# The last batch of a cross-attention kernel: batch six's norms, softmax and weights two steps earlier, and the group sums dealt to the engines anew

## The chip, the core and the metric

The kernel runs on one core of a Trainium2 chip. The engines are called by the profile's names: PE multiplies matrices, DVE, ACT and POOL are the three engines for vectors, activations and general work, SP issues the transfers. The metric is the device time of one execution in microseconds (us). Three runs of the kernel before took 431.64 to 433.29 us, with a median of 432.96. The profile comes from one more execution, which took 434.03 us.

## The reference: what is computed

Eight batches of 112 queries (320 channels, 20 heads of 16) attend to 375 context rows of 512 channels, of which the last four are "prompt" rows. Beside the usual attention over the 371 text rows, each head compares the context that it has gathered with the prompt rows and mixes the four prompt values by that. All of it is float32. Cut to what matters:

```python
probs_t = softmax(q @ k_t^T * attn_scale)              # 112 x 371, per head
text_out = probs_t @ v_t
qsem = l2norm(probs_t @ text_ehs)                      # 112 x 512, per head
sem = qsem @ l2norm(ip_ehs)^T                          # 112 x 4
fused = q @ k_ip^T * attn_scale + 0.5 * sem
probs_ip = softmax(fused) * spatial_mask
out = (text_out + probs_ip @ v_ip) @ W_out + b_out + x
```

## The kernel before, in words

**Groups.** A step is one batch and one group of four heads, so a batch has five steps, g = 0 to 4. The kernel never forms the 112 x 512 rows of `qsem`. For a head with unnormalised probabilities p it needs only the norm of p @ context, which is the square root of p G p, where G is the Gram matrix of the context rows. Half of the symmetric G, with its off-diagonal part doubled, stands in the tile `u` beside the prompt columns, a column of ones and the head's values.

**One step.** `scores` (L686, PE) makes the scores of one head into a PSUM bank `ps_s`; `probabilities` takes their maximum (L709, DVE, tile `nmx`), the exponential (L712, ACT, tile `p`) and copies the four prompt scores out (L714, ACT, `ipl`), after which the bank is free. `sent` (L721, SP) moves p into the ring buffer `xg`, `transposed` (L729, DVE) turns it into `xgT`, in two halves in the last batch. `multiplied` (L748, PE) multiplies `xgT` with `u` into four banks `ps_qd`, one for each head, in 12 rounds j of four matrix products. The four heads use different quarters of the array's rows, and so run side by side. Before a group's products, `placed` (L655, POOL) copies that group's values into `u`, in three pieces; it may overwrite a piece only when the group before has used it, and the next group's products wait for it.

**Sums of a group.** What stands in a bank `ps_qd` is then used in two ways. The last 21 columns are copied to `pvs` by ACT (`value_sums` L761, or L778 inside `shared`). The first 371 are multiplied with p and summed, which gives the squared norm in `ss`. There are two ways to do that: `reduced` (L794) does it in one DVE instruction, with a short second one that reads the sum; `shared` has ACT copy the bank to memory (L779), POOL multiply (L783) and ACT sum (L787). `shared` is a generator with three pieces, so that the caller decides where each lands. In the last batch the first n heads of a group go to `shared`, the rest to `reduced`, with n = 3, 3, 2, 0 for g = 0 to 3.

**Finishing a batch.** `finish` is a generator, too. Piece 1: z squared, the larger of `ss` and that, the reciprocal of z (L835, L837, L848, DVE), and the division of the text output (L843, POOL). Piece 2: the square root on ACT (L852) and a load of ACT's table for the exponential (L853). Piece 3: reciprocal, product with the prompt sums, scaling, maximum, difference (L859 to L865, DVE, tile `fu`). Piece 4: the exponential (L869, ACT). Piece 5: sum, reciprocal and weights w (L873 to L877, DVE). Piece 6: the weights' transpose (L883, PE) and its copy (L889, ACT). Piece 7: the attention output and the weighted prompt values in one bank `ps_a` (L897, L900, PE), for batch six behind some filler products (L439). Then a copy (L910, ACT), the output projection `ps_o` (L917, PE), the sum with the residual (L928, DVE) and the transfer (L931, SP). The prompt values stand in a block diagonal matrix `bd`, which `own_channels` (L635, L638, POOL) makes out of a loaded one; `with_bias` (L808, POOL) adds the bias to the residual.

**The end of the kernel.** Batches are numbered 0 to 7. In the last batch's loop (b = 7) the pieces of `finish(6)` are interleaved with the steps: piece 1 inside step 1, piece 2 after step 1, pieces 3 and 4 after step 2, piece 5 after step 3. Batch seven is finished in two parts: its first 16 heads by the same `finish` (pieces 1 to 4 after step 3), its last four by `last_heads` (L1010 to L1057), behind step 4. `last_keys` (L560) and a last projection of queries (L344) stand ahead of step 1's products. Step 4's scores are made inside step 1, in banks of the pool `ps_qd`, and step 2's products use the same banks.

**What sets the order.** In this part every engine's order is written out by hand: an engine does its instructions in the order of the Python calls, and waits at each for what it needs. PSUM has eight banks in three pools: `ps_qd` with four, `ps_sc` and `ps_mm` with two each. A pool hands its banks out in turn, and a new tile waits until the last use of the bank's old one is over. Odd groups of the last batch take their product banks from `ps_mm` and `ps_sc`.

## Time and profile before

| | |
|---|---|
| median of three runs | 432.96 us (431.64 to 433.29) |
| profiled execution | 434.03 us, its span 432.2 us |
| mean granted PE clock | 0.991 of full speed |
| PE busy | 422.2 us (98%) |
| DVE busy | 327.5 us (76%) |
| ACT busy | 188.9 us (44%) |
| POOL busy | 110.0 us (25%) |

The span runs from the first to the last instruction of the profiled execution; about 1.8 us of that execution's time lie around it. All times of the form 409.81 are microseconds from the start of the span. In rows of a timeline the columns are start, duration, engine, line, operation, tile written and tiles read with their shapes, and how many instructions are merged in the row; in brackets stands the idle time ahead of it with what ended it. The chain of waits follows the work back from the last instruction, at each step to what released it. A view by stretches gives the busy time of each engine in each stretch, with counts in parentheses, then the granted PE clock as a share of full speed, the busy share of the DMA engines and their GB/s. The last batch's products begin at 384.65 us, and the last transfer of the result is issued at 429.36 us.

### The profile page before, as it was taken

To read this page: it belongs to the slowest core of one execution; us is meant where nothing else is said; L and a number is where in the kernel's file an instruction comes from. 1 tells how busy PE (TensorE), PEld (TensorE's weight loads), DVE (VectorE), ACT (ScalarE), POOL (GpSimd) and SP (SyncE) were. 2 spreads that over 40 slices of the span, in tenths; PEclk is the share of its full clock that TensorE was granted. 3 is DMA by queue.
4 is the path that set the end of the run, shared out by engine and by line. 5 is a ranking of instruction groups with operands and counts; after the bars stand their busy time and mean duration, and the time that the engine had idled before them with its cause. 6 is when DMAs were issued, how large, how long until landed. Compare 5 with 4: busy or idle time off the path is not lost.

```text
span 432.2 us, 13976 instructions
## 1 busy us (share of the span) xinstructions
PE 422.2 (98%) x5521; PEld 331.1 (77%) x5521; DVE 327.5 (76%) x674; ACT 188.9 (44%) x656; POOL 110.0 (25%) x274
## 2 busy tenths in 40 slices
PE   8999999999999999999999999999999999999986
PEld 8867868778777877888777877888776887788873
DVE  5038569786987879887897878897878877887872
ACT  2344342345434363336344353335434463455852
POOL 5310101112161213421160212511151120526600
PEclk9999999999999999999999999999999999999988
DMA  8676665786555865676645946566656447562200
GB/s 250 181 192 207 144 167 159 170 191 143 150 135 143 200 174 149 146 173 143 168 122 138 208 116 177 134 143 158 160 151 148 120 125 186 143 163 81 60 2 28
DMA packets 57631, 64.28 MB, mean 149 GB/s; under 512 B 18448, under 2 KB 51592, under 8 KB 57566
## 3 DMA queue, kind: packets, MB, share of 16 engines
q1 hardware_dynamic: 56934, 62.42, 57.0%
q8 instruction: 44, 0.72, 0.8%
q10 hardware_dynamic: 632, 0.96, 0.7%
q14 instruction: 21, 0.17, 0.1%
HBM read 18.67 MB, written 5.32 MB: 56 GB/s over the span
## 4 chain that ended last, share of the span: by engine, by line
PE 88%; DMA 4%; DVE 4%; ACT 2%; SPq 1%; issue 1%; DVEq 0%; ACTq 0%
PE ps_qd L748 42%; PE ps_v L578 13%; PE ps_k L544 9%; PE ps_g L502 7%; PE ps_s L686 5%; PE ps_q L344 3%; PE ps_o L962 2%; DMA xg<-p 2%; DMA vipx<-vipd 2%; DVE xgT L729 1%; PE ps_g L458 1%; PE ps_o L917 1%; DVE junk L794 1%; DMA ct<-in_ctx_dram 1%; PE ps_k L560 1%
## 5 line engine op out<-in xcount | busy, mean ns | idle before, releaser
L748 PE MATMUL ps_qd<-u,xgT 32*112 32x328 f32 (+11 forms) x3840 | 220.6, 353 | 0.6 <-DVE xgT L729 0.6
L748 PEld LDWEIGHTS ps_qd<-u,xgT 32*112 32x112 f32 x3840 | 187.9, 172 | 34.0 <-issue 10.4
L729 DVE STREAM_TRANSPOSE xgT<-xg 128x1536 f32<-128x1536 f32 (+1 forms) x45 | 119.2, 2665 | 7.6 <-DMA xg<-p 7.5
L712 ACT ACTIVATE p<-ps_s,nmx 112x371 f32<-112x371 f32 x156 | 84.9, 582 | 78.1 <-DVE nmx L709 62.0
L709 DVE TENSOR_REDUCE nmx<-ps_s 112x1 f32<-112x371 f32 x160 | 77.5, 528 | 43.8 <-PE ps_s L686 42.0
L794 DVE CUSTOM_DVE_ANT_0 junk<-ps_qd,p 112x371 f32<-112x371 f32 x146 | 79.2, 542 | 17.7 <-PE ps_qd L748 1.6
L686 PE MATMUL ps_s<-kT,qm 32*112 32x375 f32 (+1 forms) x320 | 64.9, 483 | 0.1
L655 POOL COPY u<-vr 128x64 f32<-128x64 f32 x120 | 26.0, 238 | 150.4 <-PE ps_qd L748 98.8
L578 PE MATMUL ps_v<-wv_sb,ctxT 128*128 128x384 f32 (+1 forms) x192 | 63.6, 480 | 0.0
L578 PEld LDWEIGHTS ps_v<-wv_sb,ctxT 128*128 128x128 f32 x192 | 35.2, 190 | 19.7
L544 PE MATMUL ps_k<-ctxT,wk_sb 128*128 128x371 f32 x136 | 46.3, 483 | 0.2 <-DVE ctxT L425 0.2
L761 ACT COPY pvs<-ps_qd 112x21 f32<-112x21 f32 x152 | 16.3, 190 | 63.9 <-PE ps_qd L748 62.0
L544 PEld LDWEIGHTS ps_k<-ctxT,wk_sb 128*128 128x128 f32 x136 | 24.9, 190 | 15.2 <-POOL ct L138 0.5
L502 PE MATMUL ps_g<-ctxT 128*32 128x375 f32 (+11 forms) x672 | 30.4, 333 | 0.0
L686 PEld LDWEIGHTS ps_s<-kT,qm 32*112 32x112 f32 x320 | 26.6, 170 | 4.8 <-ACT kT L551 2.0
L502 PEld LDWEIGHTS ps_g<-ctxT 128*32 128x32 f32 x672 | 27.7, 110 | 2.0
L714 ACT COPY ipl<-ps_s 112x4 f32<-112x4 f32 x140 | 23.6, 169 | 0.0
L353 DVE TENSOR_SCALAR qm<-ps_q,emask 128x224 f32<-128x224 f32 (+1 forms) x25 | 9.0, 394 | 17.5 <-PE ps_q L344 17.5
L404 DVE STREAM_TRANSPOSE ctxT<-ct 128x512 f32<-128x512 f32 x18 | 20.0, 1111 | 1.3 <-DMA ct<-in_ctx_dram 1.3
L585 ACT COPY vext<-ps_v 128x384 f32<-128x384 f32 (+1 forms) x24 | 11.3, 469 | 22.1 <-PE ps_v L578 22.1
L475 POOL TENSOR_TENSOR ug<-ug,half 128x128 f32<-128x128 f32 (+1 forms) x24 | 10.5, 449 | 32.0 <-ACT ug L474 32.0
L937 POOL TENSOR_TENSOR wv<-vip,w 112x1280 f32<-112x1280 f32 x6 | 14.8, 2466 | 14.3 <-DVE w L877 14.3
(169 smaller groups left out, 326.0 us busy)
## 6 DMA issues: line engine op xcount, KB each, us to landing
xg<-p SPq DMA_DIRECT2D x156, 162.3 KB
u<-ug SPq DMA_DIRECT2D x124, 99.0 KB
ct<-in_ctx_dram SPq DMA_DIRECT2D x24, 176.0 KB
vr<-vd SPq DMA_DIRECT2D x32, 120.0 KB
vip<-vipd SPq DMA_DIRECT2D x6, 560.0 KB
vd<-vext SPq DMA_DIRECT2D x7, 320.0 KB
vd<-vext SPq DMA_DIRECT2D x7, 160.0 KB
out_dram<-ob SPq DMA_DIRECT2D x8, 140.0 KB
```

Of the source, the lines that this page charges most:

```text
L404: nc.vector.transpose(ctxT[:, :, c * P : (c + 1) * P].rearrange("p e (j i) -> p j e i", i=RG), ct[:, some, :].rearrange("p j (k e) -> p j ...
L502: nc.tensor.matmul(ps[c][q * RG : (q + 1) * RG, j * RG - c * P : T - c * P], ctxT[:, e, j * RG : (j + 1) * RG], ctxT[:, e, j * RG : T], st ...
L544: nc.tensor.matmul(ps[:, :TT], wk_sb[:, e, i * P : (i + 1) * P], s["ctxT"][:, e, :TT], start=(e == 0), stop=(e == NE - 1),)
L578: nc.tensor.matmul(ps[:, :w], ctxT[:, e, c * P : (c + 1) * P], wv_sb[:, e, :w], start=(e == 0), stop=(e == NE - 1),)
L655: nc.gpsimd.tensor_copy(v, dealt(b, c, s["vr"][:, c * QN : (c + 1) * QN, g, :]))
L686: nc.tensor.matmul(ps[:S, :w], qm[a * RG : (a + 1) * RG, i, r, j * S : (j + 1) * S], s["kT"][a * RG : (a + 1) * RG, i, :w], start=True, st ...
L709: nc.vector.tensor_reduce(nmx, ps[:S, :TT], AX.X, ALU.max, negate=True)
L712: nc.scalar.activation(s["p", g][:, a, :], ps[:S, :TT], AF.Exp, bias=nmx)
L714: nc.scalar.copy(s["ipl"][:, groups[g][a], :], ps[:S, TT:T])
L729: nc.vector.transpose(xT[:, j : j + n].rearrange("p j (k q) -> p q j k", q=QN), xg[:, :, j * RG : (j + n) * RG].rearrange("p q (j k) -> p ...
L748: nc.tensor.matmul(banks[a][:S, j * RG : UW], xT[a * RG : (a + 1) * RG, j, :S], region(b, c)[a * RG : (a + 1) * RG, q, j * RG - c * P :], ...
L794: nc.vector.tensor_tensor_reduce(out=junk, in0=ps[:S, :TT], in1=s["p", g][:, a, :], scale=1.0, scalar=0.0, op0=ALU.mult, op1=ALU.add, accu ...
```

## The change

All edits lie in the last batch's loop, apart from one new parameter.

- `value_sums` takes an end a1, so that it can copy some of a group's heads.
- Batch six is finished earlier. Piece 1 comes at the end of step 0 instead of inside step 1. Pieces 2 to 4 come ahead of step 1's products, behind a load of the square root's table, instead of after steps 1 and 2. Piece 5, the weights, comes inside step 1 instead of after step 3.
- Step 3's scores of heads 0 and 1 are made after round 3 of step 0 instead of after round 1, and heads 2 and 3 are sent ahead of them. On DVE step 1's transposes so come between the two pairs of maxima.
- The third piece of a `shared` (the sums on ACT) comes at another place: that of batch six's last group goes ahead of the keys' copy L567 on ACT, that of step 2's group into step 3's products (after round 8).
- Step 3 gives its first head to `shared` (n = 1 instead of 0), so DVE has three of its heads to reduce instead of four, and ACT and POOL have one.
- `own_channels` (POOL) moves from the end of step 0 to the end of step 2, where it stands ahead of the copies L655 that place step 4's values. `with_bias(7)` (POOL) moves from the end of step 0 behind step 3.
- The bank for `last_keys` comes from `ps_sc` instead of `ps_mm`, so it is now the fourth product of step 1 that waits for the copy L567 of that bank.
- All four pieces 1 to 4 of batch seven's first 16 heads come in a row after step 3, with piece 5 of batch six no longer between them.

PE and SP have the same instructions as before; on PE two score products stand two rounds later. DVE has two instructions fewer, ACT two more (L779 and L787), POOL one more (L783). The number of ACT's table loads stays the same.

```diff
-    def value_sums(b, g, a0=0):
+    def value_sums(b, g, a0=0, a1=GROUP):
         s = st[b]
-        for h, ps in list(zip(groups[g], s["qd", g]))[a0:]:
+        for h, ps in list(zip(groups[g], s["qd", g]))[a0:a1]:
             nc.scalar.copy(s["pvs"][:, h, :], ps[:S, TT:UW])
...
     for g in range(NG):
         if g == 1:
-            keys3 = last_keys(b, bank(f"ps_k_{b}_{FULL}"))
+            keys3 = last_keys(b, bank(f"ps_k_{b}_{FULL}", spare=True))
             next(keys3)
             next(keys3)
             run(("q", b), None)
-            drain(late)
+            nc.scalar.preload_act_table(AF.Sqrt)
+            run(before, None, 3)
         for j, _ in enumerate(multiplied(b, g)):
-            if g == 0 and j < 2:
-                for a in ((2, 3), (0, 1))[j]:
+            if g == 0 and j in (0, 3):
+                for a in (2, 3) if j == 0 else (0, 1):
                     coming(NG - 2, a, bank(f"ps_s_{b}_{NG - 2}_{a}", spare=a > 1))
-            if g == 0 and j == 2:
-                transposed(b, 1)
-                for a in range(GROUP):
+            if g == 0 and j in (2, 3):
+                if j == 2:
+                    transposed(b, 1)
+                for a in (2, 3) if j == 2 else (0, 1):
                     sent(b, NG - 2, a)
...
             if g == 1 and j == 4:
-                run(before, lambda: finish(b - 1, bd=bd[:, 0]))
+                run(before, None)
+            if g == 3 and j == 8:
+                drain(sums)
             if 0 < g < NG - 1 and j in (QN - 1, 2 * QN - 1):
                 placed(b, g + 1, (j // QN,))
         if g == NG - 1:
             break
-        n = (3, 3, 2, 0)[g]
-        late, sums = sums, shared(b, g, n) if n else iter(())
-        next(sums, None)
+        n = (3, 3, 2, 1)[g]
+        ahead, sums = sums, shared(b, g, n)
+        next(sums)
         reduced(b, g, n)
-        value_sums(b, g, n)
-        if g == LEAD:
-            run(before, None, 2)
-        if 0 < g + 1 < NG - 1:
+        if g < NG - 2:
+            value_sums(b, g, n)
             transposed(b, g + 2)
-        placed(b, g + 1, range(NT) if g == 0 else (NT - 1,))
-        next(sums, None)
-        if g > 0:
-            drain(late)
+            placed(b, g + 1, range(NT) if g == 0 else (NT - 1,))
+            next(sums)
+            drain(ahead)
         if g == 0:
+            run(before, lambda: finish(b - 1, bd=bd[:, 0]))
+            run(("f", b - 2), None)
+        if g == 2:
             own_channels(bd)
-            with_bias(b)
-            run(("f", b - 2), None)
-        if g == 1:
-            run(before, None)
-        if g == 2:
             nc.scalar.preload_act_table(AF.Sqrt)
         if g == 3:
+            value_sums(b, g, 1, 3)
+            placed(b, g + 1, (NT - 1,))
+            drain(sums)
+            value_sums(b, g, 3)
             first = finish(b, (0, FULL * HC), bd=bd[:, 1])
-            for _ in range(2):
+            for _ in range(4):
                 next(first)
-            run(before, None)
-            next(first)
-            next(first)
+    with_bias(b)
     value_sums(b, g)
```

## The prediction

> **What bounds the kernel now.** I read the page first, its busy times and the chain of waits by engine:

> ```profile
> PE 422.2 (98%) x5521; PEld 331.1 (77%) x5521; DVE 327.5 (76%) x674; ACT 188.9 (44%) x656; POOL 110.0 (25%) x274
> PE 88%; DMA 4%; DVE 4%; ACT 2%; SPq 1%; issue 1%; DVEq 0%; ACTq 0%
> ```

> PE is busy for 98% of the span and carries 88% of the chain. So outside the last 20 us only less PE work would help, and the change takes none away. All edits lie behind 384 us, so next I asked for PE's timeline at the end of the span, where its idle time stands in brackets.

> ```profile
> 408.80 0.43 PE L748 MATMUL ps_qd<-u,xgT 32*112 32x72 f32 x3
> 409.81 4.92 PE L748 MATMUL ps_qd<-u,xgT 32*112 32x392 f32 x96 [0.58 <-DVE xgT L729]
> 416.12 0.27 PE L883 MATMUL ps_wT<-ident,w 112*80 112x112 f32 x1 [1.39 <-DVE w L877]
> 418.00 0.55 PE L900 MATMUL ps_a<-wT,bd 80*128 80x112 f32 x1 [0.19 <-ACT bT L981]
> ```

> Step 3's products end at 409.23. PE waits 0.58 for step 4's transposes, works until 414.73, then waits 1.39 for batch six's weights w, and once more before L900. Then I looked at the clock, by stretches:

> ```profile
> 410.56:413.98 3.42, 3.42 (x70) 3.42 (x66) 2.72 (x10) 1.66 (x6) 0.00 (x0) 1.00 0.02 5
> 413.98:417.39 3.41, 2.02 (x41) 1.79 (x35) 2.20 (x10) 2.38 (x7) 0.81 (x2) 1.00 0.00 0
> 417.39:424.22 6.83, 6.64 (x21) 4.10 (x20) 4.44 (x22) 4.50 (x14) 0.00 (x0) 0.50 0.00 0
> 424.22:431.04 6.82, 4.19 (x21) 2.46 (x19) 1.34 (x4) 0.74 (x3) 0.00 (x0) 1.00 0.15 44
> ```

> The last but two columns are the granted clock. Behind a stretch in which PE worked only 2.02 of 3.41 us, it is 0.50 for 6.83 us, and in these PE is busy and on the chain:

> ```profile
> 418.01 0.76 PE ps_a L900 x2
> 418.77 0.43 PE ps_a L897 x2
> 421.84 2.99 PE ps_o L917 x6
> 424.83 0.21 PE ps_a L897 x2
> 426.20 0.26 PE ps_wT L1045
> 426.47 1.08 PE ps_o L917 x4
> 428.84 0.49 DVE ob L1057
> ```

> Two L897 take 0.43 at half clock and 0.21 at full; six L917 take 2.99, four at full clock 1.08. So the 1.39 us wait costs twice: itself, and a slow tail.

> The other engines' rows around it, DVE first, then ACT, then POOL:

> ```profile
> 386.86 1.92 DVE L709 TENSOR_REDUCE nmx<-ps_s 112x1 f32<-112x371 f32 x4 [1.30 <-PE ps_s L686]
> 388.70 2.99 DVE L729 STREAM_TRANSPOSE xgT<-xg 128x768 f32<-128x768 f32 x2
> 394.86 0.25 DVE L353 TENSOR_SCALAR qm<-ps_q,emask 128x112 f32<-128x112 f32 x1
> 397.02 1.90 DVE L709 TENSOR_REDUCE nmx<-ps_s 112x1 f32<-112x371 f32 x4 [1.91 <-PE ps_s L686]
> 405.77 0.27 DVE L859 RECIPROCAL rn<-rn 112x20 f32<-112x20 f32 x1
> 407.55 0.62 DVE L865 TENSOR_TENSOR fu<-fu,mx 112x80 f32<-112x80 f32 x1
> 408.10 2.96 DVE L729 STREAM_TRANSPOSE xgT<-xg 128x768 f32<-128x768 f32 x2
> 414.76 0.17 DVE L837 TENSOR_TENSOR rn<-ss,z 112x16 f32<-112x16 f32 x1 [0.81 <-ACT shared L787]
> 415.89 0.24 DVE L859 RECIPROCAL rn<-rn 112x16 f32<-112x16 f32 x1
> 416.94 0.22 DVE L865 TENSOR_TENSOR fu<-fu,mx 112x64 f32<-112x64 f32 x1
> 417.61 0.55 DVE L794 CUSTOM_DVE_ANT_0 junk<-ps_qd,p 112x371 f32<-112x371 f32 x1 [0.45 <-ACT pvs L761]
> 420.76 0.16 DVE L1010 SCALAR_TENSOR_TENSOR z_last<-pvs 112x4 f32<-112x4 f32 x1
> ```

> ```profile
> 390.89 0.47 ACT L779 COPY shared<-ps_qd 112x371 f32<-112x371 f32 x1
> 393.66 0.47 ACT L567 COPY kT<-ps_k 128x371 f32<-128x371 f32 x1 [1.32 <-PE ps_k L560]
> 397.60 0.57 ACT L712 ACTIVATE p<-ps_s,nmx 112x371 f32<-112x371 f32 x1 [2.48 <-DVE nmx L709]
> 399.59 0.21 ACT L714 COPY ipl<-ps_s 112x4 f32<-112x4 f32 x1
> 402.73 1.28 ACT L852 ACT_TABLE_LOAD   x1
> 408.38 0.50 ACT L787 ACTIVATE shared<-shared 112x371 f32<-112x371 f32 x1
> 422.20 0.20 ACT L1020 ACTIVATE rn_last<-rn_last 112x4 f32<-112x4 f32 x1
> ```

> ```profile
> 394.25 2.09 POOL L638 TENSOR_SCALAR_AFFINE_SELECT bd<-bd 80x640 f32<-80x640 f32 x2
> 404.77 0.24 POOL L655 COPY u<-vr 128x64 f32<-128x64 f32 x1 [0.52 <-PE ps_qd L748]
> 406.18 1.90 POOL L783 TENSOR_TENSOR shared<-shared,p 112x371 f32<-112x371 f32 x2 [1.17 <-ACT shared L779]
> 409.36 0.24 POOL L655 COPY u<-vr 128x64 f32<-128x64 f32 x1 [0.52 <-PE ps_qd L748]
> ```

> **The change part by part.** I follow one delay through steps 0 to 4, then the tail.

> Scores 3_0 and 3_1 two rounds later. DVE does two of its four maxima (1.92) from 386.86 on, the transposes of L729 (2.99), then the other two maxima from about 390.6. DVE's sum up to step 2's transposes is the same, so these end near 395.0 as before. But an exponential starts 0.58 behind its maximum (L712 at 397.60, L709 at 397.02) and four with their copies take 2.2 (L712 to the end of L714), so those of 3_0 and 3_1 end at about 392.2. The copies of step 0's sums stand behind them in ACT's queue: they began at 390.8 (the first L779 at 390.89) and now begin at 392.2, about 1.3 for three pairs and a single one. Two L787 (0.5 each) follow, now ahead of the keys' copy L567: it starts at about 394.5, not 393.66. It frees the bank of step 1's fourth product, which so starts at 395.0; before, the copy that freed a product's bank ended at 394.13. That is 0.8 later. The other three heads use other rows of the array and go on; the fourth lags by 0.8 and sets the end of the step. The p of step 3 leave SP earlier for 3_2 and 3_3, and those transfers have over 5 us to spare: nothing.

> Pieces 2 to 4 ahead of step 1's maxima. ACT loads the square root's table behind L567 (1.28 by the row of L852) until 396.1, roots, and loads the exponential's until 397.7. DVE has z2, rn, zr and qm done by 395.8 (qm 0.7 later than at 394.86, still ahead of the scores that need it), waits for the root until 396.4, and does L859 to L865. That took 2.4 us at 405.77, beside POOL's L783, and 1.3 at 415.89, with no L783 beside it; POOL has no L783 at that time in the new order either, so I take 1.3: done at 397.7, with 2.4 as the other end. The four maxima behind it then start at 397.8 instead of 397.02, as do step 4's exponentials; the last L714 ends at 400.6, not 399.80. It frees the bank of step 2's fourth product: late by 0.8 again, and that is the same 0.8, since the head that waits is the one that lags. Weights (piece 5) add 0.9 to DVE, ahead of step 3's transposes, which end at 404.0 with their first half at 402.5, ahead of step 2's end (L655 waits for it until 404.77): nothing.

> Step 4's transposes. DVE no longer does L859 to L865 ahead of them, so they start at about 406.1 instead of 408.10, and PE's 0.58 is gone. But the lag brings step 3's end from 409.23 to 410.0. And POOL is late next. Its L655 behind step 2 moves with the lag from 404.77 to 405.6, L783 takes 1.90 and ends at 407.7, and now `own_channels` follows: a short fill and L638, 2.09, to 410.0. Only then does L655 place step 4's first piece, until 410.2, and step 4's products wait for it. So step 4 runs from 410.2 to 415.0: later by 0.27. The bounds of this term are -0.6 (the wait goes, no lag) and +1.3 (the chain at 2.4).

> Taken from POOL at step 0: L638 and L808, worth nothing there, since POOL waits for PE then. Step 3's first head on ACT and POOL: DVE has 0.7 less, and a sum on ACT comes behind a POOL product that starts at 410.65 behind L655; the sum ends at 412.2, and rn (L837), at 414.76 before, can follow at 412.5. Square root, table (1.28) and the chain end at 414.3, the exponential at 414.5, before step 4 ends. Nothing on the path.

> The tail. Batch six's w is ready at 400.5, so L883 follows step 4 at once: 414.9 instead of 416.12. With the 0.27 inside, the wait is worth -1.47. The copies on ACT of step 4's sums start at 415.05 and that of wT is done at 415.6, and L900, with 1.4 us of PE work ahead of it, starts at 416.3 without waiting: -0.5. By then no stretch has held PE idle for long, and I take the clock as full. PE's rows from L900 to the last L917 at half clock sum to 6.8 us; by the ratios above they take 3.5: -3.3. The second `ps_a` then comes at 419.7, not 424.67. Batch seven's last heads must keep up: the first L794 starts at 415.25 instead of 417.61, L1010 at 418.4 instead of 420.76, L1020 at 418.8 (422.20), and 2.4 us from there to w_last as before, 421.2. PE has its `ps_a` and ACT the copy at 421.2 as well; so L1045 moves from 426.20 to 421.2, and the rest is unchanged.

> [...]

> Sum: 0.27 - 1.47 - 0.5 - 3.3 = -5.0 us. On the profiled execution's own 434.03 this gives **429.0 us**. That execution stands 1.07 above the median, and I take the sum from it, not from the median: the runs shown lie between 431.64 and 434.03, and the slow stretch, which need not fall alike in each execution, is worth more than that spread. The new kernel should be without it, so against the median I expect -3.9 us (-0.9%).

> **The rivals.** The clock stays at half in the tail, because the gap was not its cause or because a slow stretch starts for another reason (in the new order PE may still wait near 421). Then -3.3 falls away: 434.03 - 1.7 = 432.3. For it: only one drop of that kind is in the trace. Against: it follows the only long gap.

> The moved chain takes 2.4 us as at 405.77, since POOL's L843 and L655 run beside it. All later terms shift by 1.1: 430.1.

> It gets slower: POOL becomes the bound before step 4. L655 now stands behind L783 and `own_channels`, 4.2 us in a row; spans on POOL are rough. If they take longer beside DVE's transposes, PE stands idle between 410.0 and L655, and once that gap comes near 1.39, step 4 itself may run at half clock, 3.4 more for one stretch. From 2.7 us of delay on POOL on, the kernel is slower than 435.1; at twice the duration it takes 429.0 + 4.2 + 3.4 = 436.6. Against: both durations are steady in the trace.

> **How the numbers follow.** What a measurement here can tell from no change is about 0.5%, 2.2 us: faster is below 430.8, slower above 435.1. I give the sum 0.59, the slow chain 0.15 (both faster), the half clock 0.17 (same), POOL 0.09 (slower). The range goes from 427.6 (step 4's term at its lower end gives 428.1, and 0.5 less if PE's wait near 421 goes, too) to 432.6, which takes in the half clock.

> **What would show it.** Granted clock 1.00 from 417 to 424. No wait of L883 for w. Step 4's products wait for POOL's L655, not for DVE, and start at 410.2. L567 at 394.5, and step 4's maxima at 397.8. L1045 near 421.2. The prediction is wrong if the clock falls again, if step 4 starts later than 411, or if L883 waits for ACT or DVE.

## The result, and the profile after

The changed kernel takes 429.94 us (median of six executions, 429.65 to 431.01), the kernel before beside it 432.40 (six, 431.64 to 433.29). The ratio is 0.9946, with a 95% interval of 0.9927 to 0.9966: 0.5% faster, by 2.5 us. The prediction was 429.0 us with a range of 427.6 to 432.6. So the time and the direction came out. Several of the terms behind them did not, as will be seen.

The profiled execution of the changed kernel took 429.75 us, with a span of 428.0 and a mean granted clock of 0.999. The page's busy times and its chain of waits by engine:

```profile
PE 419.5 (98%) x5521; PEld 330.3 (77%) x5521; DVE 327.8 (77%) x672; ACT 189.7 (44%) x659; POOL 111.1 (26%) x275
PE 90%; DVE 3%; ACT 3%; DMA 1%; issue 1%; POOL 0%; DVEq 0%; ACTq 0%
```

PE is busy for 2.7 us less with the same 5521 products. By the rows below that is the clock: from L900 to the end of the sixth L917 PE now needs 3.90 us (416.12 to 420.02), and needed 6.83 before. The timeline of the last 20 us, PE's rows and the sum with the residual, L1057:

```profile
383.81 1.78 PE L748 MATMUL ps_qd<-u,xgT 32*112 32x392 f32 x11
...
409.87 4.90 PE L748 MATMUL ps_qd<-u,xgT 32*112 32x392 f32 x96 [0.25 <-POOL u L655]
414.70 0.29 PE L883 MATMUL ps_wT<-ident,w 112*80 112x112 f32 x1
416.12 0.47 PE L900 MATMUL ps_a<-wT,bd 80*128 80x112 f32 x2
418.15 1.87 PE L917 MATMUL ps_o<-wo_sb,aT 128*112 128x320 f32 x6
421.82 0.26 PE L1045 MATMUL ps_wT<-ident,w_last 112*16 112x112 f32 x1 [0.83 <-DVE w_last L1040]
424.51 0.49 DVE L1057 TENSOR_TENSOR ob<-ps_o,bd 112x320 f32<-112x320 f32 x1 [2.43 <-PE ps_o L1053]
```

The last batch's products begin at 383.81 us here and at 384.65 in the profile of before. The change touches nothing ahead of them, so these 0.84 us are a difference between two executions, and from here on I measure from the first product. L1057 stood 44.19 us behind it before (428.84 - 384.65) and stands 40.70 behind it now: the change is worth 3.49 us inside this pair of executions, not the forecast 5.0.

L883 and L900 wait for nothing any more. Six L917 take 1.87 us instead of 3.06. PE has a new wait, 0.83 us, for `w_last`. The view by stretches shows the clock (its last three columns: clock, DMA share, GB/s):

```profile
420.33:423.74 3.41, 2.58 (x15) 1.57 (x14) 1.16 (x5) 1.39 (x5) 0.00 (x0) 1.00 0.13 42
423.74:427.15 3.41, 0.67 (x2) 0.15 (x2) 0.49 (x1) 0.00 (x0) 0.00 (x0) 1.00 0.14 42
```

It is full up to 427.15 us, past PE's last product (L1053, to 424.42). The wait of 0.83 us leaves 2.58 us of PE work in its stretch of 3.41, and no half clock follows.

What sets the end now is in the chain of waits, which before was made of PE's rows. It runs through ACT, POOL and DVE (columns: start, duration, what; merged pieces with their count):

```profile
406.45 1.49 ACT shared L787 x6
...
407.96 1.28 ACT L1326
...
409.26 1.10 ACT shared L787 x4
...
410.42 0.37 ACT shared L779
...
410.87 0.98 POOL shared L783
...
411.88 0.60 ACT shared L787 x2
...
412.81 0.19 DVE rn L837
...
413.55 0.46 DVE fu L861
...
414.04 0.80 DVE fu L862
...
415.37 0.26 ACT ex L869
...
415.72 0.54 DVE junk L794
...
421.44 0.25 DVE w_last L1040
...
421.82 0.26 PE ps_wT L1045
```

From top to bottom: five sums on ACT with a table load between them hold up the copy L779 of step 3's first head, so POOL multiplies it at 410.87 and its sum ends at 412.48. Only then come batch seven's norms and softmax, its exponential at 415.37, the copies of step 4's sums on ACT behind that, the first L794 of the last four heads at 415.72, and the last heads' own chain to `w_last`. PE had finished step 4 at 414.77 already.

### The profile page after: what moved, and what is told of

The parts are those of the page before. It is cut to its first block, busy times and chain, and to the rows that moved or that the text cites. A ratio compares the mean times of both kernels' runs of the same rounds, so it can differ in the third digit from the quotient of the medians.

```text
span 428.0 us, 13975 instructions
## 1 busy us (share of the span) xinstructions
PE 419.5 (98%) x5521; PEld 330.3 (77%) x5521; DVE 327.8 (77%) x672; ACT 189.7 (44%) x659; POOL 111.1 (26%) x275
## 4 chain that ended last, share of the span: by engine, by line
PE 90%; DVE 3%; ACT 3%; DMA 1%; issue 1%; POOL 0%; DVEq 0%; ACTq 0%
PE ps_qd L748 43%; PE ps_v L578 15%; PE ps_k L544 10%; PE ps_g L502 7%; PE ps_s L686 5%; PE ps_q L344 3%; PE ps_o L962 2%; PE ps_g L458 1%; DVE junk L794 1%; ACT shared L787 1%; DMA xg<-p 1%; DVE nmx L709 1%; DMA ct<-in_ctx_dram 1%; PE ps_k L560 1%; PE ps_c L417 1%
## 5 line engine op out<-in xcount | busy, mean ns | idle before, releaser
L748 PE MATMUL ps_qd<-u,xgT 32*112 32x168 f32 (+11 forms) x3840 | 221.7, 353 | 0.3 <-POOL u L655 0.3
L748 PEld LDWEIGHTS ps_qd<-u,xgT 32*112 32x112 f32 x3840 | 189.0, 172 | 33.7 <-issue 10.4
L729 DVE STREAM_TRANSPOSE xgT<-xg 128x1536 f32<-128x1536 f32 (+1 forms) x45 | 119.3, 2672 | 6.7 <-DMA xg<-p 6.7
L712 ACT ACTIVATE p<-ps_s,nmx 112x371 f32<-112x371 f32 x156 | 84.8, 582 | 74.8 <-DVE nmx L709 63.5
L709 DVE TENSOR_REDUCE nmx<-ps_s 112x1 f32<-112x371 f32 x160 | 77.5, 529 | 42.2 <-PE ps_s L686 41.3
L794 DVE CUSTOM_DVE_ANT_0 junk<-ps_qd,p 112x371 f32<-112x371 f32 x146 | 79.2, 542 | 17.4 <-PE ps_qd L748 1.4
L686 PE MATMUL ps_s<-kT,qm 32*112 32x375 f32 (+1 forms) x320 | 65.5, 484 | 0.1
L655 POOL COPY u<-vr 128x64 f32<-128x64 f32 x120 | 25.9, 238 | 152.4 <-PE ps_qd L748 100.9
L761 ACT COPY pvs<-ps_qd 112x21 f32<-112x21 f32 x151 | 16.3, 190 | 62.3 <-PE ps_qd L748 61.9
L686 PEld LDWEIGHTS ps_s<-kT,qm 32*112 32x112 f32 x320 | 26.7, 170 | 4.8 <-ACT kT L551 2.0
L714 ACT COPY ipl<-ps_s 112x4 f32<-112x4 f32 x140 | 23.5, 168 | 0.0
L353 DVE TENSOR_SCALAR qm<-ps_q,emask 128x224 f32<-128x224 f32 (+1 forms) x25 | 9.0, 394 | 17.1 <-PE ps_q L344 17.1
L475 POOL TENSOR_TENSOR ug<-ug,half 128x128 f32<-128x128 f32 (+1 forms) x24 | 10.5, 450 | 31.9 <-ACT ug L474 31.9
```

Source lines behind the costliest of these rows:

```text
L655: nc.gpsimd.tensor_copy(v, dealt(b, c, s["vr"][:, c * QN : (c + 1) * QN, g, :]))
L686: nc.tensor.matmul(ps[:S, :w], qm[a * RG : (a + 1) * RG, i, r, j * S : (j + 1) * S], s["kT"][a * RG : (a + 1) * RG, i, :w], start=True, st ...
L709: nc.vector.tensor_reduce(nmx, ps[:S, :TT], AX.X, ALU.max, negate=True)
L712: nc.scalar.activation(s["p", g][:, a, :], ps[:S, :TT], AF.Exp, bias=nmx)
L714: nc.scalar.copy(s["ipl"][:, groups[g][a], :], ps[:S, TT:T])
L729: nc.vector.transpose(xT[:, j : j + n].rearrange("p j (k q) -> p q j k", q=QN), xg[:, :, j * RG : (j + n) * RG].rearrange("p q (j k) -> p ...
```

## The experiments

Each kernel is read in two ways: by its time beside the kernel before on the same chip, and, since single executions of one kernel differ by 1 to 2 us, by its trace from the last batch's first product. The last two columns of the table hold the start of step 4's copies L761 (ACT, four in a row) and of L1057, in us behind that product. Where a row names a clock, the trace is of an execution with that clock; the median is of executions of both kinds.

| kernel | median us (executions) | ratio, interval | L761 | L1057 |
|---|---|---|---|---|
| before, clock half in the tail | 432.40 (6) | | 32.77 | 44.19 |
| changed | 429.94 (6) | 0.9946, 0.9927 to 0.9966 | 31.72 | 40.70 |
| changed, again | 430.48 (12) | 0.9939, 0.9916 to 0.9962 | 31.68 | 40.66 |
| before with filler products | 431.15 (12) | 0.9967, 0.9946 to 0.9989 | 32.77 | 41.69 |
| only batch six moved | 431.06 (12) | 0.9951, 0.9926 to 0.9976 | 32.76 | 41.68 |
| own_channels early | 430.08 (12) | 0.9943, 0.9922 to 0.9964 | 31.53 | 40.50 |
| keys' copy first | 430.21 (10) | 0.9934, 0.9900 to 0.9967 | 31.62 | 40.59 |
| no head shared in step 3 | 430.44 (10) | 0.9939, 0.9912 to 0.9966 | 31.28 | 40.25 |
| block and bias early | 430.05 (10) | 0.9932, 0.9902 to 0.9962 | 31.09 | 40.01 |
| block, bias and sums early | 428.38 (4) | 0.9895, 0.9836 to 0.9954 | 30.19 | 39.36 |
| the same again | 428.61 (9) | 0.9911, 0.9879 to 0.9942 | 30.45 | 39.62 |
| gap put back, clock half | 431.69 (12) | 0.9992, 0.9959 to 1.0024 | 32.45 | 44.91 |
| the same, clock full | | | 32.31 | 41.52 |

The theory ahead of them was the prediction's: the gap ahead of L883 causes the half clock, and the half clock is most of what there is to win. The rival was that the order of the work brings the gain, and that the clock falls for reasons of its own.

**The changed kernel once more**, as the measure for the others on that chip.

> The changed kernel itself, as the measure for the runs beside it. It took 429.94 us in the median where the kernel before took 432.4. Expected: 429.6 to 430.4, granted clock 1.00 from 417 us on until PE is done.

It took 430.48 us, a little above the expected range, and its trace agrees with the first one to 0.04 us.

**The kernel before, with the gap filled.** The only edit is six filler products in the bank that L883 is about to write:

```diff
             ps = bank(f"ps_wT_{b}")
+            if b == B - 2:
+                warm(ps, 6)
             nc.tensor.transpose(
```

> The kernel before, with six filler products (0.11 us for each of their two passes, 1.3 us together) into the bank of the weights' transpose, ahead of it. PE is busy where it stood idle for 1.39 us; everything waits for w as before. Theory (the gap causes the slow clock): the wait for w stays, the granted clock in the tail is 1.00, the rows of L917 take 0.27 each and not 0.50, and the time falls by 1.5 to 2.6 us, to 430 to 431. Rival (the clock falls for another reason): the clock is 0.50 for 6.8 us all the same, and the time stays within 0.5 us of the kernel before.

It took 431.15 us. By stretches, and PE's rows:

```profile
414.46:417.87 3.41, 3.12 (x32) 2.71 (x26) 2.53 (x11) 2.38 (x11) 0.81 (x2) 1.00 0.00 0
417.87:421.29 3.42, 3.36 (x18) 2.29 (x19) 2.91 (x15) 2.55 (x7) 0.00 (x0) 1.00 0.02 5
```

```profile
416.03 0.26 PE L885 MATMUL ps_wT<-ident,w 112*80 112x112 f32 x1
417.93 0.47 PE L902 MATMUL ps_a<-wT,bd 80*128 80x112 f32 x2 [0.35 <-ACT bT L983]
423.64 0.26 PE L1047 MATMUL ps_wT<-ident,w_last 112*16 112x112 f32 x1 [0.83 <-DVE w_last L1042]
```

The transpose (L885 here, two lines further down) comes no earlier than before: 31.45 us behind the first product, against 31.47. The clock stays at 1.00, and L1057 comes 2.50 us earlier all the same. It stays so in all twelve executions: none has a mean granted clock below 0.998, while 21 of the 35 executions of the kernel before beside them have 0.992 or less. So the half clock followed from PE's gap. But 2.50 is not the forecast 3.3: with PE at full clock, PE waits 0.83 us for `w_last`.

**Batch six alone.** The kernel before, with batch six's pieces and the sums of its last group moved as in the change, and batch seven's four pieces so in a row, but nothing else of it:

```diff
             run(("q", b), None)
             drain(late)
+            nc.scalar.preload_act_table(AF.Sqrt)
+            run(before, None, 3)
...
-                run(before, lambda: finish(b - 1, bd=bd[:, 0]))
+                run(before, None)
...
-        if g == LEAD:
-            run(before, None, 2)
...
+            drain(late)
+            run(before, lambda: finish(b - 1, bd=bd[:, 0]))
             run(("f", b - 2), None)
-        if g == 1:
-            run(before, None)
...
-            for _ in range(2):
+            for _ in range(4):
                 next(first)
-            run(before, None)
-            next(first)
-            next(first)
```

> The kernel before with one part of the change: batch six's pieces 1 to 5 at their new places (with the sums of its last group ahead of them), and batch seven's four pieces in a row. Step 3 is reduced on DVE alone, own_channels and the bias stay at step 0, the scores and banks as before. Theory (the gap at w and the clock carry the gain): as fast as the changed kernel within 0.5 us, 429.5 to 430.4. Rival (the sums dealt anew carry a share): slower than the changed kernel by 1 us or more.

It took 431.06 us, not the expected 429.5 to 430.4. PE no longer waits for w, the clock is full, and L1057 stands at 41.68 us, where it also stands in the old order with filler products (41.69; there the line is L1059). First the rows of the kernel with filler products, then those of this one:

```profile
417.35 0.39 ACT L761 COPY pvs<-ps_qd 112x21 f32<-112x21 f32 x4
426.27 0.49 DVE L1059 TENSOR_TENSOR ob<-ps_o,bd 112x320 f32<-112x320 f32 x1 [2.38 <-PE ps_o L1055]
...
417.39 0.39 ACT L761 COPY pvs<-ps_qd 112x21 f32<-112x21 f32 x4
426.31 0.49 DVE L1057 TENSOR_TENSOR ob<-ps_o,bd 112x320 f32<-112x320 f32 x1 [2.37 <-PE ps_o L1053]
```

This says that the removed wait is worth nothing by itself once the clock is full: the two kernels start L761 at 32.77 and 32.76 us, and in all kernels with a full clock and the wait for `w_last`, L1057 follows L761 by 8.92 to 8.98 us. The changed kernel's further 1 us must come from the other edits, those that bring L761 from 32.76 to 31.72. By the traces that is the rival's 1 us: the theory, that the gap and the clock carry the whole gain, did not hold.

**`own_channels` in step 0**, where POOL is idle, instead of behind step 2:

```diff
                 if j == 2:
+                    own_channels(bd)
                     transposed(b, 1)
...
-            own_channels(bd)
             nc.scalar.preload_act_table(AF.Sqrt)
```

> The changed kernel with own_channels (2.3 us on POOL) inside step 0, where POOL stands idle, instead of ahead of the copies that place step 4's values. Theory: step 4's products no longer wait for POOL and start 0.5 to 0.8 us earlier against the start of the last batch; but ACT takes up step 4's banks only behind the exponential of batch seven's first heads (415.37 us), which does not hang on PE, so the end moves by less than 0.3 us. Rival (POOL's place is what the change lost): the whole 0.5 to 0.8 us is gained at the end, about 429.2.

It took 430.08 us. Step 4's products no longer wait for POOL, and the last one ends 0.7 us earlier (L883, which follows it on PE, starts at 30.17 instead of 30.89 us from the first product). L1057 gains only 0.2. Here, PE has 1.3 us to spare between the end of step 4 and the copies of its sums:

```profile
414.23 0.29 PE L883 MATMUL ps_wT<-ident,w 112*80 112x112 f32 x1
415.42 0.26 ACT L869 ACTIVATE ex<-fu 112x64 f32<-112x64 f32 x1 [0.83 <-DVE fu L865]
```

**The keys' copy ahead of the sums**, to take the lag of L567 out (piece 1 of batch six, which needs the sums, moves with them):

```diff
         if g == 1:
...
+            drain(ahead)
             nc.scalar.preload_act_table(AF.Sqrt)
-            run(before, None, 3)
+            run(before, lambda: finish(b - 1, bd=bd[:, 0]), 4)
...
-            drain(ahead)
+            if g > 0:
+                drain(ahead)
         if g == 0:
-            run(before, lambda: finish(b - 1, bd=bd[:, 0]))
```

> The changed kernel with one order undone: ACT copies the last keys (L567) ahead of the two sums of batch six's last group, not behind them. Measured from the last batch's first product, the changed kernel starts step 4 at 26.05 us and the sum with the residual L1057 at 40.7. Theory (prediction): the 0.8 us by which L567 is late is one lag that is carried from step to step, and step 2's bank, freed by the last L714 behind the two table loads, sets the same lag again; so step 4 still starts at 25.9 to 26.1, L1057 at 40.6 to 40.8, time unchanged within 0.3 us. Rival: the lag of L567 is the cause of step 4's late start; step 4 starts at 25.3 to 25.5, and the time falls by up to 0.5 us.

It took 430.21 us. L567 and step 4 in its timeline:

```profile
392.78 0.47 ACT L567 COPY kT<-ps_k 128x371 f32<-128x371 f32 x1
409.79 4.90 PE L748 MATMUL ps_qd<-u,xgT 32*112 32x392 f32 x96 [0.25 <-POOL u L655]
```

The copy is 0.9 us earlier, but step 4 still starts 25.96 us behind the first product instead of 26.06. The last L714, which frees step 2's fourth bank, gains no more than that: it ends 16.28 us behind the first product, in the changed kernel 16.38. So the lag comes back at the next bank, as the theory had it.

**Step 3 dealt as before**, all four heads reduced on DVE:

```diff
-        n = (3, 3, 2, 1)[g]
-        ahead, sums = sums, shared(b, g, n)
-        next(sums)
+        n = (3, 3, 2, 0)[g]
+        ahead, sums = sums, shared(b, g, n) if n else iter(())
+        next(sums, None)
...
-            value_sums(b, g, 1, 3)
+            value_sums(b, g, 0, 3)
```

> The changed kernel with the dealing of step 3 undone: all four heads are reduced on DVE, none goes to ACT and POOL. With the clock held full by filler products the kernel before reaches the first L794 of the last heads 32.96 us after the last batch's first product, the changed kernel 31.9. Theory: this 1.05 us comes from the place of the sums on ACT (third pieces now ahead of the end of step 3), not from the head dealt anew, since DVE's fourth reduction ends before ACT's sum of that head would; first L794 at 31.5 to 31.9, time unchanged or lower by up to 0.4 us. Rival: the dealing is what brings it; first L794 at 32.6 to 33.0 and the time 0.7 to 1.0 us above the changed kernel's.

It took 430.44 us, which the changed kernel's 430.48 cannot be told from, and in the trace L1057 stands 0.45 us earlier. So the head given to ACT and POOL in step 3 brings nothing; by the trace it costs about 0.4 us. That leaves the place of the sums as what brings L761 forward against the kernel with only batch six moved. There, the chain of waits has step 2's two sums ahead of batch seven's norms:

```profile
414.21 1.00 ACT shared L787 x4
...
415.24 0.19 DVE rn L837
```

In the changed kernel they are made inside step 3, which is one us less ahead of L837. L837 starts 29.00 us behind the first product in the changed kernel and 30.61 there, 1.61 earlier; 0.57 of this is lost again at L862 (next experiment), and 1.04 is what L761 gains. This is by exclusion and from that row: neither this edit nor the new order of step 3's scores and the new bank of `last_keys` was run alone.

**POOL's pieces and the sums.** First both of POOL's pieces in step 0, then the three sums of step 1's group inside step 2 as well:

```diff
                 if j == 2:
+                    own_channels(bd)
+                    with_bias(b)
                     transposed(b, 1)
...
-            own_channels(bd)
             nc.scalar.preload_act_table(AF.Sqrt)
...
-    with_bias(b)
     value_sums(b, g)
```

> The changed kernel with both of POOL's moved pieces (the block diagonal matrix, L635 and L638, and the residual with the bias, L808) in step 0 of the last batch, where POOL is idle. Theory: L862 takes 0.79 us in the changed kernel because POOL's L808 runs beside it; without it L862 takes 0.23 (as in the kernel before), the exponential of batch seven's first heads starts 0.5 us earlier, and everything behind it too: L1057 at 40.1 to 40.3 us from the last batch's first product instead of 40.7, time 0.4 to 0.6 us below the changed kernel's. Rival: the durations are L862's own at this place; it stays at 0.8 and the time as it is.

It took 430.05 us, and L1057 comes 0.69 us earlier, 0.49 of it beyond the run with `own_channels` alone. The timeline of the changed kernel around batch seven's softmax, POOL and DVE:

```profile
413.29 0.63 POOL L843 TENSOR_TENSOR attn<-pvs,zr 112x256 f32<-112x256 f32 x1 [1.44 <-ACT rn L852]
413.55 0.45 DVE L861 TENSOR_TENSOR fu<-pvs,rn 112x64 f32<-112x64 f32 x1
413.88 0.86 POOL L808 TENSOR_TENSOR bd<-x_sb,bias_sb 112x320 f32<-112x320 f32 x1
414.04 0.79 DVE L862 SCALAR_TENSOR_TENSOR fu<-fu,ipl 112x64 f32<-112x64 f32 x1
```

The same rows in the kernel with both pieces in step 0:

```profile
413.84 0.63 POOL L843 TENSOR_TENSOR attn<-pvs,zr 112x256 f32<-112x256 f32 x1 [1.45 <-ACT rn L852]
414.10 0.45 DVE L861 TENSOR_TENSOR fu<-pvs,rn 112x64 f32<-112x64 f32 x1
414.59 0.22 DVE L862 SCALAR_TENSOR_TENSOR fu<-fu,ipl 112x64 f32<-112x64 f32 x1
```

With L808 gone from beside it, L862 takes 0.22 us instead of 0.79. Only a fill (L888) runs beside it here. The median lies 0.4 us below that of the changed kernel's twelve executions, less than single executions differ by; the trace carries this point.

Then the sums as well:

```diff
-            if g == 3 and j == 8:
+            if g in (2, 3) and j == 8:
                 drain(sums)
```

> As the run with both of POOL's pieces early, and the sums on ACT of step 1's group (three L787) are made inside step 2, after its round 8, instead of behind step 3. Theory: with the granted clock full, the end hangs on the chain from batch seven's first 16 norms to its exponential and the copies of step 4's sums; three L787 of 0.5 us less ahead of it on ACT let the first L794 of the last heads start about 1.0 us earlier than in the changed kernel (31.9 us from the last batch's first product), bounded by the end of step 4's products; L1057 at 39.5 to 39.8 us, time 1.0 to 1.2 us below the changed kernel's. Rival: DVE's reductions or the end of step 4 hold the chain; L1057 at 40.1 or later, as in the run without the moved sums.

It took 428.38 us in four executions. All of them lie below the fastest of the changed kernel, which was not run beside it. The chain of waits is PE's again, but for one sum with the residual (L928):

```profile
404.96 8.75 PE ps_qd L748 x174
413.71 0.23 PE ps_wT L883
```

L761 starts 30.19 us behind the first product, where step 4's products end (404.96 + 8.75 = 413.71). There the end of step 4 is the bound, and the rest of the chain on ACT and DVE is hidden. Once more, for a narrower interval:

> The kernel with both of POOL's pieces and the sums of step 1's group moved early, once more, for a narrower interval: 428.0 to 428.8 us, ratio 0.988 to 0.992, and no execution with a mean granted clock below 0.997.

It took 428.61 us (427.86 to 429.87), ratio 0.9911 (0.9879 to 0.9942): this version is faster than the kernel before. The changed one was not run beside it; against that it gains 1.1 to 1.3 us by the traces (L1057 at 39.36 and 39.62 instead of 40.70) and 1.3 to 2.1 us by the medians.

**The gap put back.** The changed kernel, with batch six's weights made behind batch seven's four pieces:

```diff
-            if g == 1 and j == 4:
-                run(before, None)
...
             for _ in range(4):
                 next(first)
+            run(before, None)
     with_bias(b)
```

> The changed kernel with the weights w of batch six (piece 5, three DVE instructions, 0.9 us) made behind batch seven's four pieces instead of in step 1, all else as changed: PE then waits about 1.7 us for w between step 4's products and L883, as it waited 1.39 us in the kernel before. Theory: it is such a gap that brings the stretch of 6.83 us at half clock, and not in every execution, since the clock's stretches lie differently in each; the mean granted clock is 0.983 to 0.992 in 3 to 9 of the 12 or so executions (before: 32 of 60, changed: none of 18), these take 433.5 to 436 us, and the others 431.0 to 432.0, since w stands 0.9 us ahead of the last heads on DVE and the second ps_a comes about 1.8 us later on PE. Rival: the clock's stretch belongs to the old order of the last batch; then it stays at 0.998 to 1.0 in all of them.

Four of its twelve executions have a mean granted clock of 0.991 or 0.992 and take 434.19 to 435.22 us; the other eight take 430.41 to 432.03. The one profiled is of the first kind: behind a stretch with 1.90 us of PE work the clock falls to half.

```profile
414.77:418.18 3.41, 1.90 (x27) 1.68 (x21) 2.73 (x12) 1.76 (x9) 0.44 (x2) 1.00 0.00 0
418.18:425.01 6.83, 6.83 (x21) 4.14 (x20) 3.64 (x19) 2.96 (x7) 0.00 (x0) 0.50 0.00 0
```

The kernel before does the same: of its 80 executions beside three groups of these runs, 40 have a mean clock of 0.992 or less, with a median of 433.96 us, and 40 have more, with a median of 431.5. Of these 40, eight show 0.996. By an estimate (half of 3.41, over 430), one stretch of 3.41 us at half clock lowers the mean over 430 us by 0.004, so these may have lost one stretch; none of them was profiled. None of the 97 executions of the kernels without such a gap (the other rows of the table) went below 0.998. To see why it is about half of the executions, I profiled both kernels with a gap once more.

> The kernel before, unchanged, for a second profile. Half of its executions show no stretch of 6.83 us at half clock. Theory: the clock is set for whole stretches of 3.41 us that run freely, by how long PE worked in the one before; the gap of about 1.4 us brings the half clock only where it lies inside one stretch (2.0 of 3.41 us worked: half clock follows), and not where a stretch's border cuts it (over 2.5 of 3.41 us worked on either side; the changed kernel kept its clock behind 2.58). So in this profile the border, read from the clock's later change, either cuts the gap and the clock stays at 1.00, or it doesn't and the clock falls to 0.50 at the next border. Rival: the granted clock does not go by the border; a gap inside one stretch without a slow one behind it, or a cut gap with one.

> The changed kernel with the gap put back (w of batch six behind batch seven's four pieces), for a second profile: 4 of its 12 executions showed the half clock, the one profiled among them. Theory: as for the kernel before; where a border of the 3.41 us stretches cuts the gap of 1.5 us into parts of under about 0.9 us, the clock stays at 1.00 and the sum with the residual L1057 comes about 41.7 us behind the last batch's first product; where not, it falls to 0.50 for 6.83 us and L1057 comes at about 44.9. Rival: as for the kernel before.

The kernel before took 433.83 us. By stretches, its gap (414.58 to 415.96) lies inside the first one, and half clock follows:

```profile
413.73:417.14 3.41, 2.03 (x45) 1.81 (x37) 2.26 (x11) 2.38 (x7) 0.81 (x2) 1.00 0.00 0
417.14:423.97 6.83, 6.73 (x22) 4.18 (x21) 4.38 (x21) 4.59 (x14) 0.00 (x0) 0.50 0.00 0
```

The kernel with the gap put back took 430.44 us. Its gap is as long as in the other profile, 1.51 us, but the border of the stretches at 415.37, as I read it from the clock's later change, cuts it:

```profile
411.96:415.37 3.41, 2.59 (x72) 2.47 (x64) 2.69 (x10) 1.87 (x5) 1.64 (x3) 1.00 0.00 0
415.37:418.79 3.42, 2.73 (x23) 2.46 (x24) 2.70 (x11) 2.10 (x9) 0.00 (x0) 1.00 0.00 0
```

The gap itself, in PE's timeline of this execution:

```profile
416.06 0.27 PE L883 MATMUL ps_wT<-ident,w 112*80 112x112 f32 x1 [1.51 <-DVE w L877]
```

It leaves 2.59 and 2.73 us of work in the two stretches, and the clock stays at 1.00, up to 425.61, where the view ends. The same program, the same gap of 1.51 us, and L1057 at 41.52 us instead of 44.91. So the theory held in both profiles. It rests on one gap that a border cut by this reading and, with the earlier profiles, on three that none cut.

## Why the prediction was right, and where it was wrong

**The clock in the tail (-3.3): right in its cause, mis-sized.** The run with filler products, set against the profile of before with its half clock, puts it at 2.50 us. PE's own rows from L900 to the sixth L917 got shorter by 2.9 (6.83 to 3.90), where 3.3 was forecast. The rest goes to a wait: the step "Batch seven's last heads must keep up" let them do so, but they are 0.83 us late, so the faster PE runs into them.

And only half of the executions of the kernel before pay it whole. The prediction said that the slow stretch need not fall alike in each; 32 of the 80 show a mean clock of 0.999 or more, and eight 0.996, by the estimate above half of it. So the change is worth about 3.5 us against an execution with the half clock and about 1 us against one without (41.69 to 40.70 in the traces, the first with filler products), and the measured medians differ by 2.5, in between.

A wait of 1.38, 1.39 or 1.51 us was enough for the half clock, where it lay inside one stretch of 3.41 us: in the two profiles of before and in the first one of the gap put back.

**The wait for w (-1.47) and the one ahead of L900 (-0.5): gone, but worth nothing on their own.** Both rows show no wait. But the kernel that has only lost these waits ends where the one ends that has kept them behind filler products. At full clock, the end does not hang on PE there.

**Step 4 (+0.27): mis-sized, hidden by another chain.** Measured from the first product, step 4 starts at 26.06 us; before it was 25.16, and the forecast 25.55. So it is 0.9 later. (The prediction's own figures give 0.39, not 0.27: 410.2 instead of 409.81, with the same 4.92 us behind it.) The lag is right in its first part: L567 was forecast for 394.5, which is 0.84 earlier on this clock, 393.66.

```profile
393.65 0.56 ACT L567 COPY kT<-ps_k 128x371 f32<-128x371 f32 x1
394.63 0.86 POOL L808 TENSOR_TENSOR xb<-x_sb,bias_sb 112x320 f32<-112x320 f32 x1
394.83 0.69 DVE L837 TENSOR_TENSOR rn<-ss,z 112x20 f32<-112x20 f32 x1
397.38 1.89 DVE L709 TENSOR_REDUCE nmx<-ps_s 112x1 f32<-112x371 f32 x4
407.55 2.08 POOL L638 TENSOR_SCALAR_AFFINE_SELECT bd<-bd 80x640 f32<-80x640 f32 x2
```

Step 4's maxima come 0.4 us later than forecast (396.96 on this clock), since DVE's norms stand beside POOL's work: L837 takes 0.69 us with 20 heads, where it took 0.18 with as many before (at 399.13). POOL's `own_channels` then ends at 409.63 instead of 409.2, and step 4 waits for L655, as forecast. That this costs next to nothing here is what the run with `own_channels` early shows: 0.7 us less on PE, 0.2 at the end. But it is only hidden. On PE's own path the sixth L917 ends 36.21 us behind the first product, before 40.18: 3.97 earlier and not 5.0, since 0.6 is missing at step 4 and 0.4 at the clock. By these rows the forecast would have been missed by about 1.0 us all the same, had the chain below kept up.

**The step that failed: "the sum ends at 412.2, and rn (L837) ... can follow at 412.5. ... the exponential at 414.5, before step 4 ends. Nothing on the path."** On this clock that exponential was forecast for 413.7. It came at 415.37, 1.7 us late, behind step 4's end, and it was on the path. Two things were left out. The sum of step 3's first head ended at 412.48 instead of 411.4: the forecast had POOL's product start when POOL was free of L655 (410.65, or 409.8 on this clock), but POOL waited until 410.87 for the copy L779, which stood on ACT behind five sums and a table load. And the chain from L859 to L865 took 2.07 us instead of the 1.3 that I carried over from 415.89 in the profile of before, because L843 and the moved L808 ran beside it on POOL: "with_bias" had been given a price only at the place that it left. As the copies of step 4's sums stand behind this exponential on ACT, the first L794 of the last heads came at 415.72, where 414.41 had been forecast, and the 1.3 us go through to the end. This is nearly all of the missing 1.5 (5.0 - 3.49): L1045, forecast for 420.36 on this clock (421.2), came at 421.82.

Two runs confirm both: L808 away brings 0.5 us, and three sums less ahead of L779 another 0.4 to 0.65, until PE is the bound again.

**The rivals.** The half clock that stays was wrong for this kernel. A remark beside the sum, that the slow stretch need not fall alike in each execution, is what lowers the gain in the median from 3.5 to 2.5. The chain of 2.4 us: batch six's took 1.64, between the two ends, without a cost at the end. POOL as the bound: step 4 does wait for POOL, for 0.25 us, and is not on the path. So the time came out 0.94 us from the forecast, and part of that is luck. The terms were 1.5 us too good; 0.84 of this was made up by a last batch that happened to begin earlier in the profiled execution of the changed kernel, which no edit touches.

## What to carry to other kernels

Before pricing a wait on PE, ask what would end last if PE never waited and never slowed: here a second chain, 8.9 us from the copies of the last sums to the result, made PE wait 0.83 us as soon as its clock was full, so the first 2.5 us were PE's and the next 1.0 was that chain's. Instructions that are moved on an idle engine have to be priced at the place that they go to, by the queue that they lengthen and by what runs beside them there. And a slow stretch of the clock seen in one profile is worth what it costs at the end of such an execution, times the share of executions that have it; take that share from the executions' granted clocks.

## What the runs showed of the hardware

In the changed kernel three DVE instructions that read two tiles of SBUF ended just after a POOL instruction that had started ahead of them and ran beside them: L837 at 395.52 with POOL's L808 ending at 395.49, L861 at 414.00 with L843 at 413.92, L862 at 414.83 with L808 at 414.74. Beside a fill, which reads no tile (L888 at 414.53, in the run with both pieces early), L862 takes 0.22, and with nothing of POOL beside it 0.23 (at 416.43 in the profile of before). So in these rows such a collision cost what was left of POOL's instruction, up to 0.57 us for one of 0.22.
